# Softmax tiles turned by 32x32 blocks on VectorE and by strip transfers instead of by TensorE

## The chip, the cores and the metric

The kernel runs on one core of a Trainium2 chip. The metric is the device time of one execution in microseconds (us). Three executions of the kernel before took 562.25, 562.4 and 562.97 us; the median is 562.4. The engines are TensorE (PE, its weight loads PEld), VectorE (DVE), ScalarE (ACT), GpSimd (POOL) and SyncE (SP), which here only issues transfers (DMAs).

## The reference

One transformer block in float32, with batch 4, 512 tokens, width 512 and 16 heads of 32 columns: the input is normalized, and attention and a feed-forward network, both of the normalized input, are added to the input.

```python
xn = _layernorm(x)
q, k, v = proj(Wq, bq), proj(Wk, bk), proj(Wv, bv)      # 16 heads of 32 columns
scores = einsum('bhqd,bhkd->bhqk', q, k) / sqrt(32) + alibi_slope * distance
scores = where(causal, scores, min)
ctx = einsum('bhqk,bhkd->bhqd', softmax(scores), v)
attn = ctx @ Wo + bo
ffn = (silu(xn @ gate.T) * (xn @ up.T)) @ down.T          # weights: cubic interpolation of control points
out = x + attn + ffn
```

The feed-forward weights are 512 x 2048 matrices that the kernel uses in a factored form, with tables that it builds while attention runs.

## The kernel before, in words

Attention fills the first 411 us of the program, the feed-forward network the rest. Attention works on 64 units `(b, hg, i)`: batch `b`, a group `hg` of four heads, and a tile `i` of 128 queries. Four units, `i` = 0 to 3, make a group, numbered here g = 4b + hg (0 to 15). A loop over steps n = 0 to 66 (line 1013) handles unit n and, three steps later (`LAG`, line 29), turns it.

In step n, in program order:

- `normalize` of unit n-1: DVE takes reciprocals (L879), POOL scales the four softmax tiles (L881).
- `scores` of unit n: four matmuls on PE into four PSUM banks (L837; the matmuls for `i` = 0 and `i` = 1 are both issued in the step of `i` = 0), then four fused reductions on DVE (L850), one for each head, out of PSUM into the tile `p{i}`.
- `exponentials` on ACT (L866).
- In a step with n mod 4 = 3, `values` of the group before (L908): with g for that group, this is step 4g+7, and step 66 for the last group. For each of four key tiles c, four matmuls multiply the turned softmax tiles of key tile c with the values.
- `turn` of unit n-3 (L894): for each key tile c from 0 to `i`, four PE transposes of 128x128 into one PSUM bank, and one copy into `pT{c}`, on DVE for odd c (L897) and on ACT for even c (L899). A set of four transposes and one copy is called a set below; a group has 1+2+3+4 = 10 of them.
- `items` and `small` of the step: projections of queries (L779), keys (L779), values (L810) and of the output (L480), transposes of the next batch's input, the tables' transfers; and `some_weights`, which builds the feed-forward weights on DVE (L629, L632, L671, L674) from tables loaded by SP (L612, L615, L659).

`in_order` (line 381) ties every engine to program order, so nothing on an engine overtakes. All transfers are issued by SP, in program order, on one queue; a transfer that waits for an engine holds every later one. A transfer also waits until the one eight before it has completed, since eight semaphores are used in turn. A matmul of two 32-bit operands stands in the profile as two records; a transpose stands as one.

The tiles `p{i}` and `pT{c}` have one buffer each; the PSUM pool `mm` of the turns and projections has three banks, that of the scores four.

Of the kernel before, what the change touches and what calls it, by code (L numbers as in the profile page):

```python
# [12 lines left out]
F32 = mybir.dt.float32  # L13
# [5 lines left out]
P = 128  # L19
# [4 lines left out]
NB = D // P  # L24
NTT = B * NB
NG = 4
NHG = H // NG
NEG = -3.0e38
LAG = 3
BIG = 3.4e38  # L30
SLOPES = [2.0 ** (-8.0 / H * (h + 1)) for h in range(H)]

# [11 lines left out]
Q32 = 32  # L44
# [352 lines left out]
def block_kernel(  # L397
# [17 lines left out]
    nc = tc.nc  # L415
# [127 lines left out]
    with ExitStack() as att:  # L543
# [4 lines left out]
        tp = att.enter_context(tc.tile_pool(name="turn", bufs=1))  # L548
# [14 lines left out]
        for k in range(2):  # L563
# [24 lines left out]
            out=dist[:, S - P :],  # L588
            in_=dist[:, S - P :],
# [232 lines left out]

        units = [(b, hg, i) for b in range(B) for hg in range(NHG) for i in range(NB)]
        soft, pT, banks = {}, {}, {}

        def scores(u):


            b, hg, i = u
            nk = (i + 1) * P  # L830
            if i != 1:

                banks[b, hg] = [ps_s.tile([P, S], F32, name="s") for _ in range(NG)]
                for k, at in ((0, 0), (1, P)) if i == 0 else ((i, 0),):
                    for j in range(NG):
                        rows = slice(j * HD, (j + 1) * HD)
                        nc.tensor.matmul(  # L837
                            banks[b, hg][j][:, at : at + (k + 1) * P],
                            lhsT=qk[b, hg, "q"][rows, k * P : (k + 1) * P],
                            rhs=qk[b, hg, "k"][rows, : (k + 1) * P],  # L840
                            start=True,
                            stop=True,
                        )
            at = P if i == 1 else 0
            ps = [bank[:, at : at + nk] for bank in banks[b, hg]]
            p = sp.tile([P, NG, nk], F32, name=f"p{i}")
            low = stat.tile([P, NG], F32, name="low")
            total = stat.tile([P, NG], F32, name="sum")
            for j in range(NG):
                nc.vector.tensor_tensor_reduce(  # L850
                    out=p[:, j, :nk],
                    in0=ps[j],
                    in1=dist[:, S - nk :],
                    scale=-SLOPES[hg * NG + j],
                    scalar=BIG,
                    op0=ALU.add,
                    op1=ALU.min,
                    accum_out=low[:, j : j + 1],
                )
            soft[u] = p, low, total  # L860

        def exponentials(u, heads):
            p, low, total = soft[u]
            nk = (u[2] + 1) * P
            for j in heads:
                nc.scalar.activation(  # L866
                    p[:, j, :nk],
                    p[:, j, :nk],
                    AF.Exp,
                    bias=low[:, j : j + 1],  # L870
                    scale=-1.0,
                    accum_out=total[:, j : j + 1],
                )

        def normalize(u):
            p, _, total = soft[u]
            nk = (u[2] + 1) * P
            inv = stat.tile([P, NG], F32, name="inv")
            nc.vector.reciprocal(inv, total)  # L879
            for j in range(NG):  # L880
                nc.gpsimd.tensor_scalar(  # L881
                    p[:, j, :nk], p[:, j, :nk], inv[:, j : j + 1], 1.0, ALU.mult, ALU.mult
                )

        def turn(u, c):


            b, hg, i = u
            if i == c:
                pT[b, hg, c] = tp.tile([P, NG, (NB - c) * P], F32, name=f"pT{c}")  # L890
            p = soft[u][0]
            ps = ps_m.tile([P, NG, P], F32, name="mm")
            for j in range(NG):
                nc.tensor.transpose(ps[:, j, :], p[:, j, c * P : (c + 1) * P], ident)  # L894
            out = pT[b, hg, c][:, :, (i - c) * P : (i - c + 1) * P]
            if c % 2:
                nc.vector.tensor_copy(out, ps)  # L897
            else:
                nc.scalar.copy(out, ps)  # L899

        def values(b, hg):


            ps = ps_c.tile([P, S], F32, name="c")
            for c in range(NB):
                w = pT.pop((b, hg, c))
                for j in range(NG):
                    nc.tensor.matmul(  # L908
                        ps[j * HD : (j + 1) * HD, c * P :],
                        lhsT=vals[b][:, c, hg * P + j * HD : hg * P + (j + 1) * HD],  # L910
                        rhs=w[:, j, :],
                        start=(c == 0),
                        stop=(c == NB - 1),
                    )
            if hg == 0:
                if b == B - 1:
                    ctxT[b] = wd.rearrange("p (c s) -> p c s", c=NB)
                else:
                    ctxT[b] = ctp.tile([P, NB, S], F32, name="ctxT")

            def keep_it():

                nc.scalar.activation(
                    ctxT[b][:, hg], ps, AF.Identity, bias=bcol[:, 2, hg : hg + 1]
                )

            return keep_it


        items = {n: [] for n in range(len(units) + LAG)}  # L930
        small = {n: [] for n in range(len(units) + LAG)}
        early = {n: [] for n in range(len(units) + LAG)}

# [6 lines left out]
        for b in range(B):  # L940
            at = 4 * NHG * b
# [26 lines left out]
        for b in range(B):  # L968
            at = 4 * NHG * b
# [3 lines left out]
        for b in range(B):  # L973
            copies = [lay_out(b, part) for part in range(2)]
            for n, (to, rows) in enumerate(step for part in copies for step in part):
                at = LAID_OUT[b][n % 3 == 2] + n // (3 if b < 3 else 9)
# [30 lines left out]
        def some_weights(us):  # L1007
            while weights and us > 0.0:
                cost, step = weights.popleft()
                step()  # L1010
                us -= cost

        for n in range(len(units) + LAG):
            u = units[n] if n < len(units) else None
            old = units[n - LAG] if n >= LAG else None
            if 0 <= n - 1 < len(units):
                normalize(units[n - 1])
            if u:
                scores(u)
            for step in early[n]:  # L1020
                step()
            keep_it = None
            if n % NB == NB - 1 and n >= NB + LAG:
                g = n // NB - 1
                keep_it = values(g // NHG, g % NHG)
                exponentials(u, range(NG - 1))
                keep_it()
                exponentials(u, range(NG - 1, NG))
            turns = list(range(old[2] + 1)) if old else []
            for c in turns[:1]:  # L1030
                turn(old, c)
            if u and not keep_it:
                exponentials(u, range(2))
            for c in turns[1:2]:
                turn(old, c)
            if u and not keep_it:
                exponentials(u, range(2, NG))
            budget = 0.0 if n < NB else (2.4, 2.4, 1.2, 2.4)[n % NB] - 0.6 * len(small[n])
            some_weights(0.5 * budget)
            for step in items[n]:  # L1040
                step()
            for c in turns[2:]:
                turn(old, c)
            for step in small[n]:
                step()
            some_weights(0.5 * budget)
            if old:
                soft.pop(old)
        assert not weights
        values(B - 1, NHG - 1)()  # L1050


# [27 lines left out]
    acts, inner, own, sums, res = {}, {}, {}, {}, {}  # L1080
# [78 lines left out]
    def down_values(b, tiles, pool, tag):  # L1159

        if tiles[0] == 0:
            sums[b] = [pool.tile([P, S], F32, name=tag) for _ in range(NB)]
        steps = [(g // 2, [inner[b, g], inner[b, g + 1]]) for g in tiles[::2]]
        if tiles[-1] == NRT - 1:
            steps.append((NRT // 2, 2 * [lone[b % 2]]))
        for a, values in steps:
            for r in range(NB):
                rows = slice(r * Q32, (r + 1) * Q32)
                for half, o in enumerate(values):
                    cols = slice(half * ND, (half + 1) * ND)  # L1170
                    nc.tensor.matmul(  # L1171
                        sums[b][r][cols, :],
                        lhsT=dR[rows, a, cols],
                        rhs=o[rows, :],
                        start=(a == 0),
                        stop=False,
                    )
# [118 lines left out]
```

## Time and profile before

| | |
|---|---|
| median of three executions | 562.4 us |
| profiled execution, its span | 563.4 us |
| PE busy, share of the span | 553.7 us, 98% |
| DVE busy | 355.4 us, 63% |
| ACT busy | 295.4 us, 52% |
| POOL busy | 184.3 us, 33% |
| mean DMA rate | 135 GB/s |
| mean granted TensorE clock | 0.997 |

Busy time of an engine is the time in which at least one of its instructions ran. A group's line in the profile gives its source line, engine, operation, output and inputs, the number of instructions, busy time, mean duration of one, and what ended the idle time before them. Matmuls overlap in the pipeline, so their pace is busy time over count, not the mean duration. A line of the timeline gives start, length, engine, line, operation and the number of instructions merged; in brackets, how long the engine was idle before and what it waited for.

### The profile page before, as it was taken

How to read it: one execution, taken by the hardware profiler on the slowest of the kernel's cores; microseconds unless marked ns; L12 is line 12 of the kernel's file. 1: busy time of each engine (PE TensorE's matmuls, PEld its weight loads, DVE VectorE, ACT ScalarE, POOL GpSimd, SP SyncE). 2: the span in 40 equal slices, each digit the busy share in tenths (PEclk: the TensorE clock that was granted, in tenths of full speed). 3: DMA queues.
4: the chain of work that ended last, by engine and by line, in shares of the span. 5: the costliest groups of instructions: out<-in, count | busy, mean ns of one | idle time of the engine just before them, and what ended most of it. 6: DMA issues, size and time to landing. Idle time of an engine off the chain costs nothing.

```text
span 563.4 us, 12222 instructions
## 1 busy us (share of the span) xinstructions
PE 553.7 (98%) x4524; PEld 297.0 (53%) x4524; DVE 355.4 (63%) x990; ACT 295.4 (52%) x782; POOL 184.3 (33%) x332
## 2 busy tenths in 40 slices
PE   7999999999999999999999999999999999999997
PEld 5645555554445554454555455554633674756652
DVE  5169998897687786465653554555633585765836
ACT  2266767655356656654665566676722262524323
POOL 2034535251325144231424144244411513323310
PEclk8999999999999999999999999999999999999999
DMA  8933337345636572133314001632334566555444
GB/s 293 352 85 74 76 78 225 75 95 142 195 104 205 179 247 82 29 95 114 101 32 146 24 1 31 208 90 48 99 101 152 171 239 216 169 174 174 172 153 163
DMA packets 36667, 76.17 MB, mean 135 GB/s; under 512 B 5920, under 2 KB 5920, under 8 KB 36096
## 3 DMA queue, kind: packets, MB, share of 16 engines
q1 hardware_dynamic: 36608, 75.40, 42.7%
q8 instruction: 35, 0.57, 0.4%
q14 instruction: 24, 0.20, 0.1%
HBM read 50.74 MB, written 23.68 MB: 132 GB/s over the span
## 4 chain that ended last, share of the span: by engine, by line
PE 86%; DVE 6%; ACT 4%; DMA 3%; issue 1%; SPq 0%; DVEq 0%
PE mm L779 17%; PE mm L894 11%; PE mm L810 9%; PE g L1070 9%; PE mm L480 7%; PE s L837 6%; PE o L1171 6%; PE c L908 5%; PE o L1117 4%; PE o L1188 3%; PE o L480 3%; ACT p L866 2%; PE mm L508 2%; DVE p L850 2%; PE o L1070 2%; PE g L1117 1%
## 5 line engine op out<-in xcount | busy, mean ns | idle before, releaser
L881 POOL TENSOR_SCALAR p<-p,inv 128x128 f32<-128x128 f32 (+3 forms) x256 | 141.9, 573 | 259.5 <-DVE inv L879 245.4
L866 ACT ACTIVATE p<-p,low 128x128 f32<-128x128 f32 (+3 forms) x256 | 140.7, 552 | 47.7 <-DVE low L850 47.5
L850 DVE CUSTOM_DVE_ANT_0 p<-s,dist 128x128 f32<-128x128 f32 (+3 forms) x256 | 109.2, 482 | 36.5 <-PE s L837 35.6
L894 PEld LDWEIGHTS mm<-ident,p 128*128 128x128 f32 x640 | 71.0, 141 | 41.0 <-issue 25.7
L894 PE MATMUL mm<-ident,p 128*128 128x128 f32 x640 | 89.2, 278 | 1.6 <-ACT pT L899 0.7
L899 ACT COPY pT<-mm 128x512 f32<-128x512 f32 x96 | 55.2, 580 | 52.9 <-PE mm L894 52.6
L1093 POOL COPY made<-inner 128x512 f32<-128x512 f32 x64 | 39.0, 633 | 98.5 <-DVE inner L1092 68.6
L1070 PE MATMUL g<-feat,wT 32*64 32x512 f32 x864 | 66.7, 592 | 0.0
L1085 ACT ACTIVATE act<-g 128x512 f32<-128x512 f32 x64 | 33.0, 603 | 57.4 <-PE g L1070 57.1
L810 PE MATMUL mm<-wv,xnT 128*128 128x512 f32 x128 | 59.5, 607 | 1.9 <-ACT xnT L764 1.9
L779 PE MATMUL mm<-xnT,wk 128*128 128x512 f32 (+1 forms) x136 | 59.3, 579 | 0.5 <-ACT xnT L764 0.2
L779 PE MATMUL mm<-xnT,wq 128*128 128x512 f32 (+1 forms) x136 | 58.0, 569 | 0.3 <-ACT pT L899 0.2
L837 PE MATMUL s<-kT,qT 32*128 32x512 f32 (+3 forms) x512 | 51.0, 468 | 0.3
L897 DVE COPY pT<-mm 128x512 f32<-128x512 f32 x64 | 43.6, 686 | 8.9 <-PE mm L894 8.4
L866 ACT ACTIVATION_READ_ACCUMULATOR p<-p,low 128x1 f32 x256 | 48.4, 189 | 0.0
L1070 PEld LDWEIGHTS g<-feat,wT 32*64 32x64 f32 x864 | 32.4, 131 | 20.0 <-issue 8.6
L1092 DVE TENSOR_TENSOR inner<-g,act 128x512 f32<-128x512 f32 x44 | 27.3, 684 | 22.8 <-PE g L1070 16.7
L480 PE MATMUL mm<-ctxT,wo 128*128 128x512 f32 x88 | 40.0, 597 | 0.0
L1171 PE MATMUL o<-inner,dRM 32*64 32x512 f32 x512 | 38.2, 588 | 0.0
L779 PEld LDWEIGHTS mm<-xnT,wk 128*128 128x128 f32 x136 | 24.5, 189 | 25.5 <-issue 21.9
L908 PE MATMUL c<-pT,v 128*32 128x128 f32 (+3 forms) x512 | 37.8, 436 | 0.0
L810 PEld LDWEIGHTS mm<-wv,xnT 128*128 128x128 f32 x128 | 23.4, 193 | 26.1 <-issue 23.8
(100 smaller groups left out, 572.5 us busy)
## 6 DMA issues: line engine op xcount, KB each, us to landing
feat<-table SPq DMA_DIRECT2D x16, 512.0 KB
inner<-made SPq DMA_DIRECT2D x32, 256.0 KB
table<-samples SPq DMA_DIRECT2D x64, 88.0 KB
xp<-in_xp_dram SPq DMA_DIRECT2D x16, 256.0 KB
samples<-xnT SPq DMA_DIRECT2D x4, 1024.0 KB
feat<-in_coef_dram SPq DMA_DIRECT2D x8, 512.0 KB
feat<-in_rowpts_dram SPq DMA_DIRECT2D x32, 128.0 KB
xt<-in_xT_dram SPq DMA_DIRECT2D x16, 256.0 KB
```

The lines of the kernel that those rows point to most:

```text
L480: nc.tensor.matmul(ps, lhsT=wsb["o"][:, c, r * P : (r + 1) * P], rhs=ctxT[b][:, c, :], start=(c == 0), stop=(c == NB - 1),)
L779: nc.tensor.matmul(ps[0][:, tokens], lhsT=wsb[name][:, c, hg * P : (hg + 1) * P], rhs=xnT[b][:, c, tokens], start=(c == 0), stop=(c == NB ...
L810: nc.tensor.matmul(ps[0], lhsT=xnT[b][:, c, t * P : (t + 1) * P], rhs=wsb["v"][:, c, :], start=(c == 0), stop=(c == NB - 1),)
L837: nc.tensor.matmul(banks[b, hg][j][:, at : at + (k + 1) * P], lhsT=qk[b, hg, "q"][rows, k * P : (k + 1) * P], rhs=qk[b, hg, "k"][rows, : ( ...
L850: nc.vector.tensor_tensor_reduce(out=p[:, j, :nk], in0=ps[j], in1=dist[:, S - nk :], scale=-SLOPES[hg * NG + j], scalar=BIG, op0=ALU.add, ...
L866: nc.scalar.activation(p[:, j, :nk], p[:, j, :nk], AF.Exp, bias=low[:, j : j + 1], scale=-1.0, accum_out=total[:, j : j + 1],)
L881: nc.gpsimd.tensor_scalar(p[:, j, :nk], p[:, j, :nk], inv[:, j : j + 1], 1.0, ALU.mult, ALU.mult)
L894: nc.tensor.transpose(ps[:, j, :], p[:, j, c * P : (c + 1) * P], ident)
L899: nc.scalar.copy(out, ps)
L908: nc.tensor.matmul(ps[j * HD : (j + 1) * HD, c * P :], lhsT=vals[b][:, c, hg * P + j * HD : hg * P + (j + 1) * HD], rhs=w[:, j, :], start= ...
L1070: nc.tensor.matmul(ps[k][cols, :], lhsT=wT[rows, q, 2 * w + part, cols], rhs=feat[b][rows, q, part, :], start=(part == 0), stop=(part == 1),)
L1171: nc.tensor.matmul(sums[b][r][cols, :], lhsT=dR[rows, a, cols], rhs=o[rows, :], start=(a == 0), stop=False,)
```

## The change

Only key tiles 0 and 2 are still turned by PE, with the copies on ACT. For key tiles 1 and 3 a new function `swap`, run for unit n-2 in step n, transposes on VectorE each 32x32 block in its place: one instruction for the four heads of one unit and key tile (128x512 elements), from the softmax tile into a tile `blocks`, stored so that what belongs to one strip of 32 partitions lies together. A group has four such instructions (`SLOTS`: unit 1, unit 2 and unit 3 for key tile 1, unit 3 for key tile 3). After the group's last unit, in step 4g+5, SP issues 16 transfers, each of 32 partitions by 2048 bytes (64 KB), from strip a of `blocks` to strip r of `moved`; they move each block to its strip of partitions. `values` reads key tiles 1 and 3 from `moved`, with a moving operand that consists of runs of 32 elements. `blocks` and `moved` have one buffer each. The sets of key tile 2 come before the `items` of the step, where before they came behind them.

```diff
+LAG_SWAP = 2
+SLOTS = [(1, 1), (2, 1), (3, 1), (3, 3)]
...
         def turn(u, c):
...
-            out = pT[b, hg, c][:, :, (i - c) * P : (i - c + 1) * P]
-            if c % 2:
-                nc.vector.tensor_copy(out, ps)
-            else:
-                nc.scalar.copy(out, ps)
+            nc.scalar.copy(pT[b, hg, c][:, :, (i - c) * P : (i - c + 1) * P], ps)
+
+        def swap(u):
+            b, hg, i = u
+            if i == 1:
+                blocks[b, hg] = tp.tile([P, NB, len(SLOTS), NG, Q32], F32, name="blocks")
+            own = blocks.get((b, hg))
+            for slot, (at, c) in enumerate(SLOTS):
+                if at == i:
+                    nc.vector.transpose(
+                        own[:, :, slot].rearrange("p r j k -> p j r k"),
+                        soft[u][0][:, :, c * P : (c + 1) * P].rearrange(
+                            "p j (r k) -> p j r k", k=Q32
+                        ),
+                    )
+            if i == NB - 1:
+                moved[b, hg] = to = tp.tile([P, NB, len(SLOTS), NG, Q32], F32, name="moved")
+                for step in range(NB):
+                    for a in range(NB):
+                        r = (a + step) % NB
+                        nc.sync.dma_start(
+                            out=to[r * Q32 : (r + 1) * Q32, a],
+                            in_=own[a * Q32 : (a + 1) * Q32, r],
+                        )
+                blocks.pop((b, hg))
 
         def values(b, hg):
             ps = ps_c.tile([P, S], F32, name="c")
+            swapped = moved.pop((b, hg)).rearrange("p a s j k -> p s a j k")
             for c in range(NB):
-                w = pT.pop((b, hg, c))
+                if c % 2:
+                    slots = [s for s, (_, of) in enumerate(SLOTS) if of == c]
+                    w = swapped[:, slots[0] : slots[-1] + 1]
+                    part = lambda j: w[:, :, :, j]
+                else:
+                    w = pT.pop((b, hg, c))
+                    part = lambda j: w[:, j]
                 for j in range(NG):
                     nc.tensor.matmul(
...
-                        rhs=w[:, j, :],
+                        rhs=part(j),
...
-            turns = list(range(old[2] + 1)) if old else []
+            turns = list(range(0, old[2] + 1, 2)) if old else []
...
-            for c in turns[1:2]:
+            for c in turns[1:]:
                 turn(old, c)
             if u and not keep_it:
                 exponentials(u, range(2, NG))
+            if 0 <= n - LAG_SWAP < len(units):
+                swap(units[n - LAG_SWAP])
...
-            for c in turns[2:]:
-                turn(old, c)
```

More of the change, by code (lines that the diff above doesn't have):

```diff
@@ L824, in block_kernel @@
         soft, pT, banks = {}, {}, {}
+        blocks, moved = {}, {}
         def scores(u):
```

## The prediction

> **What bounds the kernel now.** I read the page's busy times first, then busy times by stretch of attention, the groups of the lines that the change removes, the timeline around one group's `values`, SP's own timeline, and the granted clock.
>
> ```profile
> PE 553.7 (98%) x4524; PEld 297.0 (53%) x4524; DVE 355.4 (63%) x990; ACT 295.4 (52%) x782; POOL 184.3 (33%) x332
> ...
> L894 PE MATMUL mm<-ident,p 128*128 128x128 f32 x640 | 89.2, 278 | 1.6 <-ACT pT L899 0.7
> ...
> L897 DVE COPY pT<-mm 128x512 f32<-128x512 f32 x64 | 43.6, 686 | 8.9 <-PE mm L894 8.4
> ```
>
> ```profile
> 44.00:140.00 96.00, 95.10 (x574) 49.57 (x572) 85.02 (x228) 59.40 (x171) 39.87 (x64) 1.00 0.42 111
> 140.00:230.00 90.00, 89.04 (x474) 45.11 (x475) 64.57 (x204) 50.83 (x148) 32.16 (x56) 1.00 0.50 159
> 230.00:320.00 90.00, 89.88 (x525) 45.99 (x524) 49.04 (x177) 52.25 (x147) 28.86 (x56) 1.00 0.28 85
> 320.00:411.00 91.00, 90.30 (x603) 48.66 (x610) 47.41 (x172) 59.98 (x173) 35.51 (x68) 1.00 0.27 81
> ```
>
> The columns are the stretch, its length, busy PE, PEld, DVE, ACT, POOL, clock, DMA share and GB/s. PE has no gap of note in any quarter of attention, so work taken off PE is worth its pace, unless a wait takes its place. The transposes run at 89.2/640 = 0.139 us each. DVE is next, at 89% in the first quarter.
>
> Where the new wait would stand is read from the timeline; here for group 12, from the scores of step 52 at 343.74 to the group's `values` in step 55 (lines of other work left out):
>
> ```profile
> 343.74 0.94 PE L837 MATMUL s<-kT,qT 32*128 32x128 f32 x16
> ...
> 349.84 0.17 DVE L879 RECIPROCAL inv<-sum 128x4 f32<-128x4 f32 x1
> ...
> 350.93 0.42 DVE L850 CUSTOM_DVE_ANT_0 p<-s,dist 128x256 f32<-128x256 f32 x1
> ...
> 361.57 2.36 PE L908 MATMUL c<-pT,v 128*32 128x512 f32 x32
> ```
>
> In step 4g+5 the `swap` of the group's last unit follows the last reduction of the 256-column unit. So VectorE can begin it 7.6 us after the start of the scores of step 4g+4 (at 351.3), and PE reaches `values` 17.8 us after it. Between these two moments, 10.2 us here, the two last block transposes and all 16 transfers have to fit.
>
> SP's price for such transfers stands in the feed-forward stage, where L1106 issues copies within SBUF of the very same shape, 32 partitions by 2048 bytes:
>
> ```profile
> L1106 SPq DMA_DIRECT2D lone<-lone x12: 551/588/1453, 450.3 to 549.9; - x12
> ```
>
> ```profile
> 450.32 1.86 SPq L1106 DMA_DIRECT2D lone<-lone  x3
> ```
>
> Issue takes 0.588 us (median; the columns are minimum, median, maximum in ns), and three in a row take 1.86, a pace of 0.62. In the trace's completion records these 12 land 1.94 to 3.33 us after issue, median 2.03.
>
> The clock is read from the start of the program:
>
> ```profile
> 7.10:10.50 3.40, 1.51 (x6) 0.79 (x5) 2.47 (x10) 0.68 (x2) 0.00 (x0) 1.00 1.04 395
> 10.60:13.90 3.30, 3.30 (x8) 1.76 (x7) 2.67 (x11) 0.79 (x2) 0.00 (x0) 0.50 1.06 380
> 14.00:20.00 6.00, 5.76 (x28) 4.40 (x27) 1.33 (x4) 1.07 (x2) 0.00 (x0) 1.00 1.02 362
> ```
>
> A stretch of 3.4 us in which PE idled 1.9 us was followed by one of 3.4 us at half clock.
>
> **What goes.** Four of ten sets per group: 16 x 4 x 4 = 256 transposes x 0.139 = 35.7 us of PE, 2.23 us per group, all of it between the start of the scores of step 4g+4 and `values`. Of DVE, 64 copies x 0.686 = 43.9 us.
>
> **What comes on DVE.** 64 block transposes of 128x512 in f32, SBUF to SBUF. No row shows one. Nearest below is the 128x512 scaling into `xn`, 0.608; nearest above, for an operation that moves twice as much, the 128x1024 sum of L632, 1.265. Same-size rows lie at 0.61 to 0.69, so I take 0.69: DVE's load stays as it was. Both ends are kept for the range.
>
> **What comes on SP.** 256 transfers, 16 per group in one train. The train is not hidden: `values` waits for all 16. From the last reduction of step 4g+5: two block transposes 1.4, semaphore 0.1, 15 paces of 0.62 = 9.3, landing of the last 2.0; together 12.8 us. `values` has only key tile 0 to do first (8 of its 32 matmul records; 17.0/16 = 1.06 us of busy time, of which I count 0.9). PE arrives 2.23 earlier than before. With R the time from the scores of step 4g+4 to the last reduction, and W the time from there to `values`, both from the timeline, the stall is X = R + 12.8 - (W - 2.23 + 0.9), or R - W + 14.1, or none:
>
> | g | 0 | 1 | 2 | 3 | 4 | 5 | 6 | 7 | 8 | 9 | 10 | 11 | 12 | 13 | 14 |
> |---|---|---|---|---|---|---|---|---|---|---|---|---|---|---|---|
> | R | 8.0 | 10.6 | 7.6 | 7.6 | 15.9 | 6.4 | 8.4 | 5.3 | 8.4 | 5.3 | 5.3 | 5.2 | 7.6 | 5.6 | 10.3 |
> | W | 15.0 | 20.7 | 17.6 | 18.2 | 29.8 | 19.0 | 18.2 | 18.2 | 24.6 | 19.0 | 17.6 | 14.5 | 17.8 | 14.9 | 15.6 |
> | X | 7.1 | 4.0 | 4.1 | 3.5 | 0.2 | 1.5 | 4.3 | 1.2 | 0 | 0.4 | 1.8 | 4.8 | 3.9 | 4.8 | 8.8 |
>
> The sum is 50.4. In some groups R contains a backlog of DVE (the first unit's reductions end later than the 2.0 us of an unloaded group, by 8.5 us in all); a PE that stalls lets DVE catch up, so I take 42. Against 15 x 2.23 = 33.5 saved, that leaves +8.5.
>
> Group 15 has no work to cover it. Now POOL finishes scaling its last tile at about 405.5 and `values` ends at 410.4. With the change, 405.5 + 0.1 + 1.4 + 9.3 + 2.0 gives 418.4, and the remaining 24 matmul records take some 1.5: 419.9, or +9.5. The feed-forward stage stands behind it on PE.
>
> **Queues.** On SP, everything behind the train is late by up to 10 us. The weight tables have some 6 to 10 us between landing and use, and PE itself stalls meanwhile, so I count nothing, up to 5 once (the load issued at 50.9 and used at 66.1). Between steps 25 and 29 SP has 12 table copies at 0.78, 14 loads at 0.45 and two larger sets, some 18.5 us, besides 9.9 for a train, in about 24: the next train starts up to 4.4 late; I take 2. On DVE, the next group's first block transpose (step 4g+7) waits for the train to have read `blocks`, with value copies and weights behind it; PE is stalled by the same train, so nothing is added.
>
> **Clock.** Six stalls (groups 0, 11, 12, 13, 14 and the end) are of 3.9 us or more, enough that some 3.4 us stretch holds 1.9 of idling. Half clock over one full stretch costs 1.7 us of matmuls: 0 to 10 us; I take 1.0 for each, 6. [...]
>
> **`values`.** Key tiles 1 and 3 are read in runs of 32 elements. No row has a moving operand in short runs; all the f32 rows keep one pace. Nothing to 15 us (twice the time for 512 of 1280 columns of 37.8 us); I take nothing, as the data per column is the same.
>
> Sum: 8.5 + 9.5 + 2 + 6 = +26 on the profiled 563.4, which lies 1.0 over the median: 588.
>
> [...] The row of L1106 has 0.588 us of issue, and the measurement decides.
>
> **The rivals.** *The train is short enough* (faster): the price per issue decides. SP's loads of 32 strips at L615 take 1.82 for four, a pace of 0.46. Then each train is 2.4 shorter, the table's 42 falls to 17, the end to 7, the clock to 2: 17 - 33.5 + 7 + 2 = -7, or 555. The change loses from about 0.50 us per issue on. For it: these loads have 32 partitions too. Against: every copy within SBUF in the trace (L1097, L1102, L1106) issues in 0.55 us or more.
>
> *A dearer path* (slower still): block transposes at twice 0.69 add 1.35 to about 13 trains, 17 us; short runs in the moving operand up to 15; the full clock price 4. All would give 624, one of the first two about 605. For it: no row of either. Against: same-size f32 rows on DVE lie within 0.1 us of each other.
>
> *No change*: stalls of exactly the 35.7 saved; it needs a pace near 0.50, which no row has.
>
> **How the numbers follow.** Late trains at the price of L1106, 575 to 602: 0.60. The dearer path, over 602: 0.17. Short trains: 0.20, no change: 0.03. Within 0.2% of 562.4 counts as no change, about what a measurement can tell. So faster 0.20, same 0.03, slower 0.77. The forecast's own range is 575 to 602; with the other cases, 551 (short trains, with 4 us off for the queues and clock) to 618 (one dear operation with the full clock and queue price).
>
> **What would show it.** Right: PE idle ahead of the matmuls that read `moved`, released by DMA, longest in groups 0, 14 and 15 and near zero in 4, 8 and 9; SP issuing 16 in 9 to 10 us; half-clock stretches behind the long stalls; L894 with 384 transposes. Wrong: an issue pace under 0.5, block transposes above 1 us, or DVE as the releaser of PE in the first quarter, where it is already at 89%.

## The result and the profile after

The changed kernel takes 634.6 us (median; 633.42 to 638.27), and the kernel before, on the same chip, 562.68. The ratio is 1.129, with an interval of 1.125 to 1.132: slower by 72 us. The forecast was 588 with a range of 551 to 618; the direction was right, and the size was far off. The profiled execution has a span of 631.6 us against 563.4, or +68.2, and a mean granted clock of 0.943 against 0.997.

The page of the kernel after: busy times, granted clock in 40 slices, the chain that ended last, and the groups of `values`, the remaining transposes and the block transposes.

```profile
PE 556.5 (88%) x4268; PEld 281.3 (45%) x4268; DVE 354.1 (56%) x990; ACT 295.3 (47%) x782; POOL 181.0 (29%) x332
...
PEclk9999889798999979989999979798688999999999
...
PE 42%; SPq 15%; DMA 6%; DVE 3%; issue 2%; ACT 2%; DVEq 0%; ACTq 0%
...
L939 PE MATMUL c<-moved,v 128*32 128x384 f32 (+1 forms) x256 | 28.6, 523 | 57.6 <-DMA moved<-blocks 57.6
...
L897 PE MATMUL mm<-ident,p 128*128 128x128 f32 x384 | 60.7, 297 | 1.5 <-ACT qT L793 1.3
...
L908 DVE STREAM_TRANSPOSE blocks<-p 128x512 f32<-128x512 f32 x64 | 43.4, 696 | 19.1 <-DMA moved<-blocks 13.5
```

PE has 256 instructions fewer and yet 2.8 us more busy time: some of its work ran at half clock. SP's queue, which does no arithmetic, is now 15% of the chain, most of it the issue of the new transfers. `values` stands idle 57.6 us for `moved`.

The stretches of attention in four parts, each ending at the end of `values` of group 3, 7, 11 and 15 (columns as in the prediction):

```profile
44.00:150.70 106.70, 88.41 (x457) 41.09 (x456) 76.18 (x207) 55.30 (x159) 35.35 (x60) 0.90 0.47 126
150.70:269.10 118.40, 104.86 (x529) 49.52 (x530) 75.49 (x230) 59.59 (x170) 35.16 (x64) 0.97 0.56 166
269.10:373.20 104.10, 96.79 (x498) 46.35 (x498) 55.12 (x207) 60.23 (x174) 35.30 (x68) 0.96 0.42 117
373.20:478.10 104.90, 75.24 (x409) 36.58 (x410) 35.83 (x130) 46.22 (x131) 27.31 (x52) 0.83 0.40 112
```

PE now idles in every part, most in the first and the last, and these are also the parts with the lowest clock.

The waits of PE and VectorE (total, times, longest), and the durations of the new operations (minimum, median, maximum in ns):

```profile
PE c L939 <- DMA moved<-blocks: 57.6, 13, 11.3
...
DVE out L525 <- DMA moments<-out: 15.3, 3, 9.2
...
DVE blocks L908 <- DMA moved<-blocks: 13.5, 7, 4.6
...
PE s L840 <- DVE low L853: 7.2, 3, 3.8
```

```profile
L919 SPq DMA_DIRECT2D moved<-blocks x256: 507/589/1923, 51.4 to 473.2; - x128
```

```profile
L908 DVE STREAM_TRANSPOSE blocks<-p x64: 661/705/712, 41.1 to 462.2; 128x512 f32<-128x512 f32 x64
```

Group 12 again, from the scores of step 52 to `values`, in the timeline of the kernel after:

```profile
378.54 0.94 PE L840 MATMUL s<-kT,qT 32*128 32x128 f32 x16
...
385.65 1.30 DVE L908 STREAM_TRANSPOSE blocks<-p 128x512 f32<-128x512 f32 x2
...
387.18 12.74 SPq L919 DMA_DIRECT2D moved<-blocks  x16
...
394.37 1.07 PE L939 MATMUL c<-pT,v 128*32 128x512 f32 x8
...
401.63 0.71 DVE L908 STREAM_TRANSPOSE blocks<-p 128x512 f32<-128x512 f32 x1 [4.64 <-DMA moved<-blocks]
...
401.69 1.51 PE L939 MATMUL c<-moved,v 128*32 128x384 f32 x8 [6.25 <-DMA moved<-blocks]
```

The order of events is the one that the prediction described: the last reduction at 385.6, two block transposes, a train of 16, and PE at `values` 15.8 us after the scores (predicted 15.6). This train is the slowest of the sixteen, 12.7 us instead of about 10, so the stall is 6.25 and not 3.9. In the trace's completion records its first six transfers, issued behind four loads of 512 KB (L542, from 385.19 on), land 4.3 to 7.4 us after issue instead of 2.0, and the third to the eighth are issued up to 1.7 us apart. The fifth to the eighth (at 390.05, 391.36, 392.68 and 394.35 us) start 0.02 us after the landing of the transfer eight before each, one of those loads.

### The profile page after: what moved, and what is told of

It is laid out like the page before. It is cut to its first block, busy times and chain, and to the rows that moved or that the text cites. A ratio compares the mean times of both kernels' runs of the same rounds, so it can differ in the third digit from the quotient of the medians.

```text
span 631.6 us, 12113 instructions
## 1 busy us (share of the span) xinstructions
PE 556.5 (88%) x4268; PEld 281.3 (45%) x4268; DVE 354.1 (56%) x990; ACT 295.3 (47%) x782; POOL 181.0 (29%) x332
## 4 chain that ended last, share of the span: by engine, by line
PE 42%; SPq 15%; DMA 6%; DVE 3%; issue 2%; ACT 2%; DVEq 0%; ACTq 0%
SPq L919 11%; PE g L1101 8%; PE o L1202 5%; PE o L1148 3%; PE mm L482 3%; PE c L939 3%; PE mm L781 3%; PE mm L897 3%; PE o L1219 2%; PE o L482 2%; DMA moved<-blocks 2%; PE mm L812 2%; PE s L840 2%; SPq L1008 2%; DVE p L853 1%
## 5 line engine op out<-in xcount | busy, mean ns | idle before, releaser
L884 POOL TENSOR_SCALAR p<-p,inv 128x128 f32<-128x128 f32 (+3 forms) x256 | 138.6, 560 | 316.8 <-DVE inv L882 264.5
L939 PE MATMUL c<-moved,v 128*32 128x384 f32 (+1 forms) x256 | 28.6, 523 | 57.6 <-DMA moved<-blocks 57.6
L1124 POOL COPY made<-inner 128x512 f32<-128x512 f32 x64 | 38.9, 633 | 112.6 <-DVE inner L1123 89.3
L840 PE MATMUL s<-kT,qT 32*128 32x512 f32 (+3 forms) x512 | 60.6, 496 | 7.8 <-DVE low L853 7.2
L897 PE MATMUL mm<-ident,p 128*128 128x128 f32 x384 | 60.7, 297 | 1.5 <-ACT qT L793 1.3
L897 PEld LDWEIGHTS mm<-ident,p 128*128 128x128 f32 x384 | 45.3, 150 | 30.2 <-issue 21.2
L908 DVE STREAM_TRANSPOSE blocks<-p 128x512 f32<-128x512 f32 x64 | 43.4, 696 | 19.1 <-DMA moved<-blocks 13.5
L840 PEld LDWEIGHTS s<-kT,qT 32*128 32x128 f32 x512 | 26.6, 198 | 40.9 <-DVE low L853 15.7
L939 PEld LDWEIGHTS c<-moved,v 128*32 128x32 f32 x256 | 9.7, 137 | 75.6 <-issue 67.2
L1101 PEld LDWEIGHTS g<-feat,wT 32*64 32x64 f32 x864 | 30.8, 133 | 21.4 <-issue 10.7
L1202 PE MATMUL o<-inner,dRM 32*64 32x512 f32 x512 | 36.4, 588 | 0.0
```

What stands on the lines that cost most here:

```text
L840: nc.tensor.matmul(banks[b, hg][j][:, at : at + (k + 1) * P], lhsT=qk[b, hg, "q"][rows, k * P : (k + 1) * P], rhs=qk[b, hg, "k"][rows, : ( ...
L884: nc.gpsimd.tensor_scalar(p[:, j, :nk], p[:, j, :nk], inv[:, j : j + 1], 1.0, ALU.mult, ALU.mult)
L939: nc.tensor.matmul(ps[j * HD : (j + 1) * HD, c * P :], lhsT=vals[b][:, c, hg * P + j * HD : hg * P + (j + 1) * HD], rhs=part(j), start=(c ...
L1101: nc.tensor.matmul(ps[k][cols, :], lhsT=wT[rows, q, 2 * w + part, cols], rhs=feat[b][rows, q, part, :], start=(part == 0), stop=(part == 1),)
L1202: nc.tensor.matmul(sums[b][r][cols, :], lhsT=dR[rows, a, cols], rhs=o[rows, :], start=(a == 0), stop=False,)
```

## The experiments

All changes are made to the kernel after, and the kernel before ran beside each (562 to 563 us). The three runs on a part of the groups, at the end, are medians of several executions; every other run is a single one, and four executions of the kernel after spread from 633.4 to 638.3 us, so differences of a few us between such runs show little.

### Full clock during the stalls

Idle matmuls into a spare bank stand ahead of the first one that reads `moved`, nearly as many as would fill the stall.

```diff
+FILL = (5, 3, 4, 4, 0, 3, 2, 1, 0, 0, 1, 4, 6, 5, 8, 12)
...
+                if c == 1 and FILL[b * NHG + hg]:
+                    spare = ps_m.tile([P, S], F32, name="mm")
+                    for k in range(FILL[b * NHG + hg]):
+                        nc.tensor.matmul(spare, lhsT=ident, rhs=vals[b][:, 0, :], start=True, stop=True)
```

> Idle matmuls (identity times values into a spare bank, 0 to 12 of 512 columns for each group, a little less than each group's wait) stand ahead of the first matmul that reads moved; nothing else changes, and the output is the same. Theory (the half clock behind each wait costs some 26 us: 53 us of matmuls ran in 71 us of half-clock stretches): PE is never idle for long, the granted clock stays near 1.00 and the span falls from 631.6 to about 606 (600 to 613). Rival (the clock matters little, the rest is DVE and queue delay): clock near 1.00, but the span within 4 us of 632.

Measured: 619.4 us, span 617.6. In the kernel after, eleven stretches at half clock make 71.4 us. The stretches' sum, from a table of windows laid on them, has PE busy for 51.1 us:

```profile
sum 71.40, PE 51.08 PEld 28.11 DVE 19.37 ACT 20.21 POOL 7.11; mean PE 4.64 PEld 2.56 DVE 1.76 ACT 1.84 POOL 0.65
```

Such work takes about twice as long as at full clock: from their start to that of the next form, the eight 128x384 matmuls of `values` took 1.25 us at half clock (63.56 to 64.81) and 0.64 at full clock (322.36 to 323.00). So about half of the 51.1 us, 25.5, is lost. Here is one of the stretches, between stretches at full clock; it begins within the stall of group 14 (444.9 to 452.2 us) and ends 5.7 us behind it:

```profile
440.00:447.70 7.70, 4.93 (x32) 2.19 (x24) 5.36 (x20) 6.20 (x19) 4.10 (x8) 1.00 0.38 88
447.70:457.90 10.20, 5.71 (x34) 3.59 (x35) 1.49 (x3) 2.49 (x6) 1.10 (x2) 0.50 0.49 139
457.90:468.10 10.20, 5.82 (x31) 2.90 (x29) 1.96 (x3) 2.06 (x4) 1.60 (x3) 1.00 0.25 74
```

With the filling, four stretches of 6.8 us are left; the same sum over them:

```profile
sum 27.20, PE 25.10 PEld 12.46 DVE 16.52 ACT 17.36 POOL 11.11; mean PE 6.27 PEld 3.11 DVE 4.13 ACT 4.34 POOL 2.78
```

That is 12.6 us lost. So the loss worked out in this way fell by 13.0 us, and the span by 14.0. The four that remain stand behind waits that were not filled, mostly the scores' for VectorE. They keep the span above the expected band of 600 to 613 us; without their 12.6 us it would be 605. The theory, that half clock behind the stalls costs far more than the 6 us of the forecast, holds.

### No transfers: what the removed work is worth

`values` reads `blocks` itself.

```diff
-                moved[b, hg] = to = tp.tile([P, NB, len(SLOTS), NG, Q32], F32, name="moved")
-                for step in range(NB):
...
-                blocks.pop((b, hg))
+                moved[b, hg] = blocks.pop((b, hg))
```

> The 16 transfers of each group are left out and values reads the block transposes where they lie, so blocks are not moved to their strips and the attention result differs. Theory (the train alone makes the waits): PE keeps what the removed transposes cost, some 32 us, no wait for a DMA is left, clock 0.99 or more, span about 531 (525 to 540). Rival (DVE or the strided operand takes a part of the loss): span over 550.

Measured: 541.7 us, span 539.9, clock 1.000, no wait for a transfer. So 256 transposes fewer give 23.5 us by the two spans (563.4 to 539.9), where the forecast had 35.7. Of these, 2.35 us lie ahead of the first scores, which the change doesn't touch: they start at 26.86 us in the profile of before, with its half-clock stretch at 10.6 us, and at 24.51 here. Beside the execution of before that ran with it, the run gains 21.3 us (562.97 to 541.72). The result lies between theory and rival, so it didn't decide why. The timelines say where some of it is. Before (two sets of unit 1 together, two of unit 2 together, two single ones around them):

```profile
74.67 0.60 PE L894 MATMUL mm<-ident,p 128*128 128x128 f32 x4
76.06 1.09 PE L894 MATMUL mm<-ident,p 128*128 128x128 f32 x8
80.93 1.04 PE L894 MATMUL mm<-ident,p 128*128 128x128 f32 x8
85.26 0.66 PE L894 MATMUL mm<-ident,p 128*128 128x128 f32 x4
```

Without transfers:

```profile
86.55 0.66 PE L897 MATMUL mm<-ident,p 128*128 128x128 f32 x4
90.48 1.04 PE L897 MATMUL mm<-ident,p 128*128 128x128 f32 x8
```

One set by itself takes 0.60 to 0.66 us, two together 1.04 to 1.09. Taking a set away from another thus gains some 0.43 us and not 4 x 0.139 = 0.56. In full groups (from the end of one `values` to the next) the run gained 1.75 us = 4 x 0.44; in groups 4, 6, 11, 13, 14 and 15, only 0.57 to 1.35.

### No transfers and no block transposes

`values` reads one constant tile for key tiles 1 and 3.

```diff
...
-                    nc.vector.transpose(
...
+            if not blocks:
+                blocks[0] = tp.tile([P, NB, len(SLOTS), NG, Q32], F32, name="blocks")
+                nc.vector.memset(blocks[0], 0.125)
+            if i == NB - 1:
+                moved[b, hg] = blocks[0]
```

> The run without transfers, with VectorE's 64 block transposes left out too: values reads one constant tile for key tiles 1 and 3 (so the output isn't the reference's). It asks why leaving out 256 transposes and 64 ScalarE copies saved 23.5 us and not 33.5. Theory A (a transpose next to another set occupies TensorE for 0.11 us, not 0.14, and that is all): the block transposes cost nothing, 538 to 542 us. Rival B (VectorE's 44 us of block transposes hold the scores back; the scores took 5.4 us more of TensorE in the run without transfers than before): 534 to 537 us, with the scores back at 48 us. Rival C (both the whole difference is VectorE's): 528 to 533 us.

Measured: 537.7 us, span 535.9. It falls between the bands of theory A and rival B, nearest A's lower end. Rival B's sign, the scores back at 48 us, did not come: their busy time is 51.0 us before, 56.4 without transfers and 56.0 here, and no run says why. PE's part of the removal is thus worth at most 25.3 us (562.99 to 537.70, the kernel before beside it), with VectorE relieved of 64 copies as well; the block transposes take 4.0 back, most of it in groups 0, 1 and 4 (2.1, 0.6 and 0.8). Of the 14.4 us by which the forecast overstated the gain (35.7 against 21.3), some 8 are the pace of a transpose in its place (16 x 0.48), up to 4 are VectorE, and the rest, in groups that gained less than 1.75, is open.

### Four transfers for sixteen

The same bytes, in four transfers of all 128 partitions, which leave the strips where they were.

```diff
-                for step in range(NB):
-                    for a in range(NB):
...
+                for r in range(NB):
+                    nc.sync.dma_start(out=to[:, r], in_=own[:, r])
```

> The same bytes in 4 transfers of 128 partitions by 2048 bytes for each group in place of 16 of 32 partitions; strips stay where they are, so blocks are not brought to their strips and the attention result differs. Theory (the number of issues at 0.62 us sets the train): it lasts about 3 x 0.65 + 3.3 = 5.3 us in place of 11.3, waits remain in groups 0, 12, 14 and at the end only, span about 545 (535 to 562). Rival (the 1 MB of each train sets its time, at the queue's rate): the waits stay, span over 610.

Measured: 550.8 us, span 549.0, clock 0.994:

```profile
PE c L934 <- DMA moved<-blocks: 7.6, 3, 4.7
```

The bytes are the same, and an issue is no shorter (median 601 ns); a landing takes 2.6 us instead of 2.0. From first issue to last landing a train takes 4.4 to 7.6 us, once 10.6, instead of 11.4 to 14.1. The number of issues makes the train long. For the same megabyte per group the kernel took 550.8 us against 634.6. It doesn't help the kernel: these four leave each block in its strip.

### The last unit turned a step earlier

```diff
-LAG_SWAP = 2
+LAG_SWAP = 1
...
-            if 0 <= n - LAG_SWAP < len(units):
-                swap(units[n - LAG_SWAP])
             budget = 0.0 if n < NB else (2.4, 2.4, 1.2, 2.4)[n % NB] - 0.6 * len(small[n])
             some_weights(0.5 * budget)
+            if 0 <= n - LAG_SWAP < len(units):
+                swap(units[n - LAG_SWAP])
```

> The block transposes and the train come one step earlier (unit n-1 in place of n-2, behind the first share of the weights); work and output are the same. Theory (each wait is what is left of the train when PE arrives): the train starts some 2 to 4 us earlier against values, the waits of groups 0 to 14 fall from 46 to some 15 to 25 us, the end's 11 stay, the half clock falls with them, span 585 to 605. Rival (DVE then waits for POOL and delays the reductions, which delays PE): the waits for moved fall, but PE waits for DVE instead, span over 620.

Measured: 644.2 us, span 642.5, clock 0.928. The rival came true. The scores' wait for VectorE rose from 7.2 to 32.9 us, and that of `values` for its trains fell from 57.6 to 22.0. Only 9.5 of the 22.0 are put down to `moved`. Two waits, of 10.4 and 2.1, are put down to other transfers, but both end 0.5 us after the last landing of the group's own train, as those for `moved` do (the 10.4 in the last group, whose train lands at 485.3 us and whose `values` go on at 485.8). PE's two longest waits, and VectorE's own:

```profile
PE s L840 <- DVE low L853: 32.9, 6, 12.4
PE c L939 <- DMA table<-moments: 10.4, 1, 10.4
...
DVE blocks L908 <- DMA moved<-blocks: 38.9, 9, 6.6
DVE out L525 <- DMA moments<-out: 37.7, 4, 15.1
DVE blocks L908 <- POOL p L884: 30.5, 17, 2.9
...
DVE wd L673 <- DMA feat<-in_downpts_dram: 25.4, 2, 14.7
```

A block transpose that waits for POOL or for the train before, and a copy whose buffer is still to be stored by a transfer behind a train, hold everything behind them on VectorE, the reductions of the scores too.

### Two queues

The transfers from odd strips are issued by ScalarE.

```diff
+                        queue = nc.scalar if a % 2 else nc.sync
-                        nc.sync.dma_start(
+                        queue.dma_start(
```

> Half of each group's 16 transfers are issued by ScalarE's queue, the other half by SyncE's; work and output are the same as in the changed kernel. Theory (the pace of issue on one queue sets the train): each queue issues 8 in 8 x 0.62, the train lasts 6.3 us in place of 11.3, waits for moved fall from 57 us to about 10 to 15 (most of it at the end), the half clock nearly vanishes, the time is about 556 (548 to 570). Rival 1 (both queues share what makes an issue slow): waits as before, over 610. Rival 2 (ScalarE, waiting for the block transposes and issuing for 5 us per group, delays the exponentials): waits for moved fall, but PE waits for ScalarE or VectorE instead, over 575.

Measured: 632.6 us, span 630.8: the second rival. Waits of PE, and the one of ScalarE:

```profile
PE c L940 <- DMA moved<-blocks: 14.8, 5, 4.4
PE mm L812 <- ACT kT L797: 9.6, 3, 4.1
PE mm L482 <- ACT kT L797: 9.3, 3, 5.8
PE c L940 <- ACT pT L898: 9.3, 4, 6.4
PE mm L897 <- ACT kT L797: 7.4, 3, 4.4
```

```profile
ACT kT L797 <- DMA moved<-blocks: 58.8, 13, 7.7
```

```profile
104.04 5.05 ACTq L920 DMA_DIRECT2D moved<-blocks  x7
109.14 0.69 ACT L797 ACTIVATE kT<-mm,bcol 128x512 f32<-128x512 f32 x1 [5.30 <-DMA moved<-blocks]
```

Each queue issues its eight in 5.0 to 6.3 us (two of the 32 in 8), where one took 10 for sixteen: the issues do not share a resource that shows. In eight of the groups one half starts 3.5 to 9.5 us behind the other, so that the train still takes 8.5 to 14.8 us to issue. And ScalarE stood idle through its queue's issues, in the lines above for 5.3 us through seven of them; in all, 58.8 us of its waits ahead of L797 are put down to these transfers, and PE waits for ScalarE's copies instead. The second queue shortened the issue, to halves of 5 us, and the time in which ScalarE stood is the price.

### Two queues, and values later; the last group by PE

In the first, `values` comes behind the projections of its step; in the second the last group is, in addition, turned by PE into the layout of `moved`; in the third that alone is done with the two queues.

```diff
+            if late:
+                g = n // NB - 1
+                values(g // NHG, g % NHG)()
+                for c in turns:
+                    turn(old, c)
+                if 0 <= n - LAG_SWAP < len(units):
+                    swap(units[n - LAG_SWAP])
```

```diff
+            if (b, hg) == (B - 1, NHG - 1):
+                return
...
-            turns = list(range(0, old[2] + 1, 2)) if old else []
+            turns = list(range(0, old[2] + 1, 1 if old[:2] == (B - 1, NHG - 1) else 2)) if old else []
```

> As with two queues, and values comes behind the projections of its step in place of ahead of them (turns and block transposes of that step behind it), so that up to 3.5 us more of PE work covers the train. Theory: no wait for moved but the end's 6 us, time about 550 (544 to 558). Rival (the later values delays what reads its result and the next turns, so the step's end is bound by ScalarE's copies): 2 us or more over the run with two queues alone.

> As the run before, and the last group, whose train nothing can cover, is turned by TensorE transposes as in the kernel before. Theory: the end's wait goes, some 5 us less than with two queues and late values, about 545 (540 to 553).

> Two queues and the last group by TensorE, with values where the change has it. Theory: some 5 us less than with two queues alone, about 551 (545 to 562); if the end's wait costs nothing (the feed-forward stage waits for something else there), no difference.

Measured: 617.1, 603.9 and 615.9 us, all far above what was expected, since ScalarE's waits for its own issues stayed at 47 to 59 us. The differences still tell something: `values` later is worth 15.5 us (632.6 to 617.1), and the last group by PE 13.3 and 16.7.

### VectorE's transfers off SP's queue

The loads of `feat` for the row-distance weights (L661) and the stores of `moments` (L528) are issued by GpSimd. What they do behind a train is seen in two timelines of the kernel after, SP's and VectorE's:

```profile
260.43 5.65 SPq L919 DMA_DIRECT2D moved<-blocks  x9
266.12 1.67 SPq L1008 DMA_DIRECT2D table<-samples  x2
...
269.19 4.60 SPq L528 DMA_DIRECT2D moments<-out  x5
```

```profile
262.76 0.69 DVE L525 COPY out<-mm 128x512 f32<-128x512 f32 x1 [0.92 <-PE mm L510]
272.63 0.68 DVE L525 COPY out<-mm 64x512 f32<-64x512 f32 x1 [9.18 <-DMA moments<-out]
```

The store of 269.19 stood behind the train (its last nine transfers are shown) and three others, VectorE's next copy waited 9.18 us for it, and the reductions behind that copy kept PE idle for 1.7 us at 273.

```diff
-                    nc.sync.dma_start(out=rows[s], in_=o[half * 64 : (half + 1) * 64])
+                    nc.gpsimd.dma_start(out=rows[s], in_=o[half * 64 : (half + 1) * 64])
...
-                        nc.sync.dma_start(out=to, in_=part)
+                        nc.gpsimd.dma_start(out=to, in_=part)
```

> The changed kernel with two kinds of transfers that VectorE waits for, the loads of feat for the row-distance weights and the stores of moments, issued by GpSimd instead of SyncE, so that they don't stand behind trains. Theory (the waits of scores for VectorE at 226 and 273 us, 7.2 us in all, and the half clock after them come from these transfers standing behind a train): the wait of scores for VectorE falls under 3 us, the half-clock stretches at 229 and 277 us go, and the time falls by 8 to 14 us, to 621 to 627 us. Rival (GpSimd is held by issuing, its normalization comes late, and the block transposes and trains with it): 632 us or more, with more waits of the block transposes for GpSimd.

Measured: 629.6 us, span 627.8, so 3.8 less and not 8 to 14, hardly clear of the kernel after's spread. The scores' wait for VectorE fell from 7.2 to 3.8 us. The half-clock stretch at 277 us went, and that at 229 shrank from 6.8 to 3.4 us (at 232, behind a wait of 1.87), but others of 3.4 us came at 188, 212 and 270 us; PE's busy time at half clock fell from 51.1 to 50.7 us only, and the wait of `values` for `moved` rose from 57.6 to 59.6. The queue causes about half of the scores' waits for VectorE, and the other half has other causes. They weren't separated further, and what the queue costs in time isn't shown.

### Only the groups without a stall

In the kernel after, groups 4, 8 and 9 never wait for `moved`. First they alone took the new path, with the other groups' tiles all copied by ScalarE into the layout of `moved`:

> Only groups 4, 8 and 9 (of 16) take the new path; the other thirteen are transposed by TensorE, all tiles of them, as in the kernel before (their tiles of key tiles 1 and 3 are copied by ScalarE into the moved layout). In the changed kernel TensorE never waited for moved in these three groups, and no other group's train runs now. Theory (a group wins what its four transpose sets cost TensorE in their place, and loses only by the wait for its own train, by the half clock after it, and by transfers queued behind it): the run without transfers saved 0.57, 1.75 and 1.75 us in these groups, so the time is 562.6 - 4.1 = about 558.5 us (557 to 561), no TensorE wait for moved, and clock 0.997. Rival (a train costs something in any group, by what it delays on SP's queue): equal to the kernel before or above it, 562 to 566 us, with a wait of VectorE for moments or feat just after one of the three trains.

Measured: 575.9 us (ratio 1.022, 1.019 to 1.025). The three groups themselves did what was expected, -2.06, -1.75 and -0.95 us against the kernel before; the other groups, without the first, lost 17 us in all, with PE waiting for ScalarE:

```profile
PE mm L813 <- ACT moved L904: 5.1, 3, 3.1
```

That was my edit and not the transfers: the kernel before copies the sets of odd key tiles on VectorE and turns key tiles 2 and 3 behind the projections, and this edit did neither. So it was repeated with the other thirteen groups as in the kernel before (its `pT1` and `pT3` share the buffer of `moved`, for space):

```diff
+MOVE = (4, 8, 9)
...
+            out = pT[b, hg, c][:, :, (i - c) * P : (i - c + 1) * P]
+            (nc.vector.tensor_copy if c % 2 else nc.scalar.copy)(out, ps)
...
+            if NHG * b + hg not in MOVE:
+                return
...
+            turns, after = [], []
+            if old:
+                turns = list(range(0, old[2] + 1, 2))
+                if NHG * old[0] + old[1] not in MOVE:
+                    turns, after = [*range(min(old[2], 1) + 1)], [*range(2, old[2] + 1)]
```

> Groups 4, 8 and 9 take the new path; the other thirteen are done as in the kernel before (four more sets of TensorE transposes copied by VectorE, in the order of the kernel before). Theory (the 576 us of the run with three groups came from ScalarE, which there had all ten copies of a group; the groups' own accounts, -2.06, -1.75 and -0.95 us, stand): no TensorE wait for moved, and 562.9 - 4 to 5 = 558 us (557 to 560). Rival (three trains on SP's queue delay other transfers, whatever the copies do): 562 us or more.

Measured: 557.5 us against 562.8, ratio 0.991 (0.990 to 0.993). It is faster than both kernels.

```profile
PE 546.6 (98%) x4476; PEld 293.4 (53%) x4476; DVE 353.9 (64%) x990; ACT 294.9 (53%) x782; POOL 184.3 (33%) x332
...
PEclk9999999999999999999999999999999999999999
```

```profile
PE c L950 <- DMA moved<-blocks: 0.6, 1, 0.6
```

Against the kernel before, groups 4, 8 and 9 are shorter by 1.97, 1.75 and 0.89 us, and group 6 by 0.61; eleven of the others keep their times to 0.01. Only group 0, with the start of the program, differs more (-2.93): there the trace of before has a half-clock stretch that this one hasn't. The new path gains what was worked out where its train fits.

### Eleven groups, values later

Groups 0 to 10 take the new path, with `values` behind the projections as in the late run above, SP alone as their queue and GpSimd for VectorE's transfers; groups 11 to 15 stay as before.

```diff
+MOVE = tuple(range(11))
...
+            late = n % NB == NB - 1 and n >= NB + LAG and n // NB - 1 in MOVE
...
+            if late:
+                g = n // NB - 1
+                values(g // NHG, g % NHG)()
+            for c in after:
+                turn(old, c)
```

> Groups 0 to 10 take the new path, with values at the end of its step, after the projections, instead of ahead of the exponentials; groups 11 to 15 are done as in the kernel before; the loads of feat for the row-distance weights and the stores of moments are issued by GpSimd. Theory (in the early groups the trains come 1 to 5 us too late for values, and nothing else is wrong with them): the waits for moved fall from 25 us in these groups to under 5, the clock stays above 0.99, and of the 11 x 1.5 = 16.5 us that the groups can save some 6 to 12 remain: 551 to 557 us. Rival (trains and copies delay VectorE, and that the scores, wherever values stand): 560 us or more, with waits of the scores for VectorE of over 5 us and several half-clock stretches.

Measured: 569.8 us (ratio 1.013, 1.010 to 1.016), span 567.2, clock 0.982. Its longest waits of PE:

```profile
PE c L950 <- DMA moved<-blocks: 7.5, 4, 3.3
PE mm L511 <- DVE xt L490: 3.9, 1, 3.9
PE s L841 <- DVE low L854: 2.6, 2, 1.7
```

Both expectations miss in part: the waits for `moved` fell from 25 to 7.5 us, not under 5, the time is 13 us above the theory's band, and the scores' wait is 2.6, not over 5. The account closes to 2 us. The run without transfers gained 18.2 us in these eleven groups; against that run PE idled 11.7 us more (18.6 against 6.9, in gaps over 0.15 us), and four half-clock stretches with 16.9 us of PE work cost some 8.5. Together +2.0; the span rose by 3.8.

## Why the prediction was wrong in size

The forecast's terms, the removed work counted whole and the end of attention before its own saving (9.5 + 2.2), beside what the runs showed:

| term | forecast, us | measured, us |
|---|---|---|
| removed transposes | -35.7 | -23.5 (run without transfers; 2.35 of it lies ahead of the first scores) |
| stalls for `moved`, groups 0 to 14 | +42 | +46.3 |
| stall for `moved`, last group | +11.7 | +11.3 |
| queues, VectorE | +2 | +8.6 (what is left of the sum) |
| half clock | +6 | +25.5 |
| sum | +26 | +68.2 |

The sum is the difference of the two profiled spans; the half-clock row is worked out from the stretches at half clock, and the run with the filling bore out about half of it.

**Right.** The step thought hardest to price came out well. A block transpose takes 0.696 us (0.69), an issue 0.589 (0.588), a landing 2.0 in the median (2.0), and a train 10.0 to 11.5, once 12.7. The stalls by group are 4.7, 3.1, 4.3, 4.2, 0, 3.3, 2.4, 1.1, 0, 0, 1.5, 3.7, 6.3, 4.4 and 7.3 for groups 0 to 14, near the table of X (sum 50.4, taken as 42 for the backlog of VectorE; 46.3 measured). Single groups miss by up to 2.4 us to both sides (group 0 predicted at 7.1, group 12 at 3.9), so a part of the sum's nearness is luck. `values` reads its runs of 32 elements at no price: the 128x384 form takes 494 ns in a stretch at full clock, and 486 before. So the "dearer path", the only rival above the forecast, is not what happened.

**Clock: "I take 1.0 for each, 6".** This step failed most, by 20 us, in the count and in the price. It counted six stalls of 3.9 us or more, though its own table of X, before any correction for VectorE's backlog, has eight groups there besides the end (0, 1, 2, 6, 11, 12, 13 and 14), and took one stretch of 3.4 us behind each. The trace has eleven stretches, behind 1.6 to 3.4 us of idling within the 3.4 us ahead of them: nine behind stalls for `moved` (groups 0 to 3 and 11 to 15) and two behind the scores' waits for VectorE (at 226 and 273 us), which the forecast left out. Six last 6.8 us and two 10.2, and the mean price is 2.3 us (25.5/11). Filling the stalls took away 13.0 of the 25.5 us worked out so, and the span followed by 14.0. The row of the start, 1.9 us of idling and then 3.4 at half clock, was on the page; it was read as a price per long stall, when it should have been asked of every stall of such length. Two of these got off: the stalls of groups 5 and 6, of 3.31 and 2.44 us, have no half clock behind them. The length of a single gap doesn't divide the cases: the stretch at 277 us came behind one of 1.71 us, and the gap of 3.31 us had none behind it.

**What goes: "256 transposes x 0.139".** Of the 35.7 us, some 21 came. The mean over all sets was taken for the price of the ones removed. A set in a row with another costs 0.43 us and not 0.56, and VectorE's block transposes, taken as a free exchange for its copies, hold PE for up to 4 us in the first groups. "DVE's load stays as it was" is true of its busy time (354.1 against 355.4 us) and says nothing of the place: the runs show the price mainly in groups 0, 1 and 4. Some 2 to 3 us stay open.

**Queues: "I count nothing", "nothing is added".** The reasoning that a PE stalled by the train hides VectorE's delay is wrong where the transfer that VectorE waits for stands behind the train: the stores of `moments` and the loads of `feat` are late after the train has ended, and the scores' reductions stand behind them. The scores waited 7.2 us for VectorE, against 1.7 without transfers. With half of this removed (transfers by GpSimd), the one execution took 629.6 us, 3.8 less than the fastest of the kernel after. The 8.6 us of the table are only what is left of the sum; how they divide between the queue, `blocks` and other waits stays open.

**The rival of short trains** was right that shorter trains make the change pay, as four issues instead of sixteen show: 550.8 us, where it gave 555. That the numbers are near is luck: it had trains of 8.9 us and 33.5 us saved on PE, and the run had trains of mostly 4.4 to 7.6 us and some 21 saved. An issue of these transfers was no cheaper with two queues (medians of 0.589 us on SP and 0.602 on ScalarE) or with four transfers (0.601).

## What to carry to other kernels

A wait added to a saturated TensorE costs its length and, often, half clock behind it: 57.6 us of waits for `moved` and 7.2 for VectorE came with some 25.5 us of slower matmuls, so price gaps of 2 us too, and not the long ones alone. Price work that goes by what its neighbours leave when it has gone, and price a train of transfers by its number of issues and by whatever else stands in its queue. A path that fits only where the schedule has room can be taken there alone: three of sixteen groups gave 5 us, where all sixteen lost 72. These three were picked from the trace of the kernel after, as those without a stall.

## What the runs showed of the hardware

- In the kernel after, the granted clock fell to 0.5 for 3.4, 6.8 or 10.2 us behind 1.6 to 3.4 us of idling within 3.4 us. Yet stalls of 3.31 us (at 207.2) and 2.44 us (at 241.5) had none behind them, nor had an idle stretch of 1.68 us in the run without transfers and one of 2.36 us in the first run with three groups. In the run with eleven groups one stretch of 3.4 us, at 217 us, came behind 0.94 us of idling. The starts of the eleven stretches (62.0, 89.3, 116.6, 147.3, 229.2, 277.0, 369.2, 399.9, 423.8, 447.7 and 468.1 us) lie whole multiples of the shortest stretch, 3.41 us, apart, to 0.1 us: 8, 8, 9, 24, 14, 27, 9, 7, 7 and 6 times. What decides whether idling is followed by half clock was not shown. The stretches of 10.2 us begin within stalls of 7.3 and 11.3 us and end 5.7 and 3.1 us behind them.
- The issue of a transfer of 64 KB within SBUF took 0.59 us on SP (kernel after) and 0.60 on ScalarE (two queues), and that of one of 256 KB 0.60 on SP (four transfers for sixteen), all medians. With two queues ScalarE stood idle for 5.3 us through seven of its issues at 104 us.
- A f32 block transpose of 128x512 on VectorE took 0.70 us (kernel after), and a copy of this size 0.69 (L897 before).
- In the first run with three groups ScalarE's copies of 128x512 from PSUM into runs of 32 elements, 2048 bytes apart, took 0.572 us, and those into whole rows 0.586 (medians).
